# Rows of the quantised FFN's scales by way of DRAM, and another plan of rounds, in a two-layer decoder on one core

## The chip, the core and the metric

The kernel runs on one core of a Trainium2 chip. The metric is the time of one execution on the device in microseconds (us), from runs of the whole kernel. A core has five engines that work side by side, each through its own list of instructions in a fixed order: PE (matrix products), DVE (vector work), ACT (activation functions and copies), POOL (a slower vector engine) and SP (here: it issues DMAs). They wait for one another by semaphores. SBUF is the memory on the chip with 128 partitions, PSUM the one that PE writes to, DRAM the memory outside.

## What is computed

The reference is a decoder of two layers on x of 32 batches x 128 tokens x 256 features. Layer 0 is self-attention, cross-attention to a context and a mixture of experts with two of eight experts per token. Layer 1 is a gated linear recurrence with an MLP (stages d and m below), attention between x and the context in both directions (stage e) and a quantised feed-forward network with a depthwise convolution (stage f). Only stage f is touched:

```python
def act_quant(x):
    scale = 127.0 / jnp.clip(jnp.max(jnp.abs(x), axis=-1, keepdims=True), 1e-05)
    return jnp.clip(jnp.round(x * scale), -128, 127) / scale
def bit_linear(x, w):                  # weight_quant makes w ternary, times a mean
    return jnp.einsum('bsd,hd->bsh', act_quant(x), weight_quant(w))
h = bit_linear(_layernorm(x), w1)      # 256 -> 1024 features
h = depthwise_conv1d(h.transpose(0, 2, 1), conv_w, conv_b)   # 3 taps along the tokens
x = x + bit_linear(silu(h.transpose(0, 2, 1)), w2)           # 1024 -> 256
```

Each token has a scale of its own, once for the input (a factor to undo it, dq) and once for the hidden features (a factor to apply, s).

## The kernel before

Layer 0 goes first, in three stages, until about 1300 us. Then `layer1` works through 16 units of two batches (U = 2, T = 256 tokens). A unit is a list of small steps (`gather`, `d_stats`, ..., `f_out`), which `PLAN` gives round numbers by hand, 0 to 89. A new unit starts every `STEP` = 11 rounds, so that at any time up to nine units are at work in different steps. The loop at the end of `layer1` writes the program round by round, older units first; within what the data allow, the framework that builds the program then orders the instructions of DVE, ACT, POOL and SP, while matrix products keep the order of the program (`mm`, `turned`: lines 206 and 209). Each engine runs its list in order: a waiting instruction holds all behind it.

In stage f tokens lie along the free axis and features on the partitions, from `f_flip` on. A scale is computed with tokens on the partitions, 128 x 2 values (`scales`, lines 1007 to 1012). To multiply by it, the kernel needs the scales of all 256 tokens in a row, the same on every partition. `on_rows` does that on PE: for each of the two batches it multiplies the column, spread over 128 columns, with the identity matrix (tile rows_f), and ACT copies the result to SBUF (rows_f_sb, line 1021).

The steps of stage f, with the lines in the profile: `f_stats`, `f_norm` (1254 to 1259, ends with the first scale), `f_quant` (1265, 1267), `f_flip` (transposes, and the first row), then four pieces of two blocks of 128 features each: `f_h` (PE products with w1, then DVE line 1277: d_f = h_f times the row), `f_z` (ACT, 1282: the middle tap with the bias), `f_taps` (DVE, 1292: the left tap, for each block; ACT, 1296: the right tap's product e_f; POOL, 1298: its sum), `f_silu` (ACT, 1305), `f_top` (DVE, 1311 and 1316: the largest values over features within a partition, two pieces at once), `f_am` (PE transposes, DVE 1323, the second scale), `f_rows` (the second row), `f_round` (DVE, 1332: z_f times the row; 1333: rounding to zi_f) and `f_out` (PE, DVE 1346, then the store of the output on SP, 1349).

Other lines that the prediction names: the recurrence has its decay scan at 1117 and its state scan at 1123, between them POOL's product u_d (1091) and DVE's u_d (1122); then POOL's qn_d (1101), DVE's pre_d (1126), POOL's pre_d (1127), DVE's pre_d (1130) and yT (1132). Norms take a power on POOL (`rsqrt`, 956: rs_d, rs_m, rs_e, rs_f) with small DVE steps before (ve, ms: 954, 1054, 1055, 1144, 1145) and after (nb, 962). ACT applies them (xn 967, hn 974) and copies transposed tiles (hT, xT: 986). POOL adds x_m to x (1147). The softmax of stage e is nm_e (1212), exp (ACT, 1217), den_e (1223), at_e (1225), then lv_e (1238) and vv_e (1199). kv_e is loaded on SP (1176).

Of the kernel before, what the change touches and what calls it, by code (L numbers as in the profile page):

```python
# [10 lines left out]
F32 = mybir.dt.float32  # L11
# [3 lines left out]
ALU = mybir.AluOpType  # L15
AX = mybir.AxisListType

P = 128
S = 128
# [56 lines left out]
def decoder(ctx: ExitStack, tc: tile.TileContext, a: dict, out: bass.AP):  # L76
    nc = tc.nc
    V, A, PE, GP = nc.vector, nc.scalar, nc.tensor, nc.gpsimd
# [8 lines left out]
    dram = ctx.enter_context(tc.tile_pool(name="scratch", bufs=1, space=bass.MemoryType.DRAM))  # L87
    psp = ctx.enter_context(tc.tile_pool(name="ps", bufs=8, space=bass.MemoryType.PSUM))

    def bank(name, dt=F32):  # L90
        return psp.tile([P, 512 if dt == F32 else 1024], dt, tag="ps", name=name)
# [22 lines left out]
    def con(name):  # L114
        at, w = C_AT[name]
        return cst[:, at : at + w]

    ident, blk, pm = con("ident"), con("blk"), con("pm")
# [86 lines left out]
    def mm(out, lhsT, rhs, start, stop):  # L205
        tc.keep_in_program_order(PE.matmul(out, lhsT=lhsT, rhs=rhs, start=start, stop=stop))  # L206

    def turned(out, in_, by=None):
        tc.keep_in_program_order(PE.transpose(out, in_, ident if by is None else by))  # L209
# [12 lines left out]
    U = 2  # L222
    T = U * S
    NU = NB // U
    ckv = dram.tile([NU, P, 2, U * D], F32, name="ckv")
    rw = keepc.tile([P, 2, NB], F32, name="rw")
    slots = keepc.tile([P, 2, NB], I32, name="slots")
    wm = keepc.tile([P, 2], F32, name="wm")
# [645 lines left out]
    def ternary(wf, keep):  # L874
# [28 lines left out]
        (29, "m_out0"), (30, "m_out1 m_out2"), (31, "m_out3"), (32, "e_stats"), (33, "e_nb"),  # L903
        (34, "e_norm"), (36, "e_flip"), (39, "e_k e_v"), (45, "e_s"), (47, "e_exp"), (48, "e_soft"),
        (50, "e_at"), (53, "e_y"), (54, "f_stats"), (55, "f_norm"), (56, "f_quant"), (58, "f_flip"),
# [4 lines left out]
    )  # L910

    def layer1(wd):
# [4 lines left out]
        w1 = wq[:, 0, :].rearrange("p (c h) -> p c h", c=2)  # L917
# [3 lines left out]
        with tc.tile_pool(name="pl", bufs=1) as pool, tc.tile_pool(name="pl1", bufs=1) as keep:  # L921
# [10 lines left out]
            def sb(tag, name, bufs=1, dt=F32, shape=(2, T)):  # L932
                return pool.tile([P, *shape], dt, tag=tag, name=name, bufs=bufs)

            def flat(t):
                return t.rearrange("p a b -> p (a b)")

            def bank3(name, n=T):
                return bank(name)[:, : 2 * n].rearrange("p (a b) -> p a b", a=2)

            def sm(tag, name, w=U, bufs=3):
                return small.tile([P, w], F32, tag=f"l_{tag}", name=f"{tag}_{name}", bufs=bufs)
# [34 lines left out]
            def flipped(src, dst, n, dt=F32):  # L977

                pt = bank(f"pt_{n}", dt)[:, : 2 * T]
                for c in range(2):  # L980
                    for i in range(U):
                        turned(
                            pt[:, c * T + i * S : c * T + (i + 1) * S], src[:, i, c * P : (c + 1) * P],
                            ident if dt == F32 else ident_b,
                        )
                A.copy(flat(dst), pt)
                return dst

            def halves(w, m, xT, name):

                p = bank3(name)
                for e in range(2):
                    for c in range(2):
                        mm(p[:, e, :], w[:, c, (m + e) * P : (m + e + 1) * P], xT[:, c, :], c == 0, c == 1)
                return p
# [9 lines left out]
            def scales(am, k, name):  # L1005

                V.tensor_scalar(am, am, 1e-5, None, ALU.max)
                s = sm(f"qs{k}", name)
                V.reciprocal(s, am)
                V.tensor_scalar(s, s, 127.0, None, ALU.mult)  # L1010
                dq = sm(f"dq{k}", name)
                V.tensor_scalar(dq, am, 1.0 / 127.0, wm[:, k : k + 1], ALU.mult, ALU.mult)
                return s, dq

            def on_rows(v, k, name):

                p = bank(name)[:, :T]
                for i in range(U):
                    mm(p[:, i * S : (i + 1) * S], v[:, i : i + 1].to_broadcast([P, P]), ident, True, True)
                r = pool.tile([P, T], F32, tag=f"rows{k}", name=f"{name}_sb", bufs=2)  # L1020
                A.copy(r, p)
                return r[:, None, :].to_broadcast([P, 2, T])

            def unit(u):
                x = X[u * U // G][:, u * U % G : u * U % G + U, :]
                d_, m_, e_, f_ = f"d{u}", f"m{u}", f"e{u}", f"f{u}"
                o = {}
# [223 lines left out]
                def f_norm():  # L1251
                    o["xf"] = xn = sb("xf", f"xn_{f_}")
                    for i in range(U):
                        V.tensor_scalar(
                            xn[:, i, :], x[:, i, :], o["mv"][:, i, 0:1], o["rs"][:, i : i + 1],
                            ALU.subtract, ALU.mult,
                        )
                    am = sm("am", f_)
                    V.tensor_reduce(am, xn, AX.X, ALU.max, apply_absolute_value=True)
                    o["s1"], o["dq1"] = scales(am, 0, f_)  # L1260

                def f_quant():
                    xn = o["xf"]
                    for i in range(U):
                        V.tensor_scalar(xn[:, i, :], xn[:, i, :], o["s1"][:, i : i + 1], MAGIC, ALU.mult, ALU.add)
                    o["xi"] = sb("xi", f"xi_{f_}", 2, BF16)
                    V.tensor_scalar(flat(o["xi"]), flat(xn), MAGIC, 127.0, ALU.subtract, ALU.min)

                def f_flip():
                    o["hT"] = flipped(o["xi"], sb("xTf", f"xT_{f_}", 2, BF16), f_, BF16)  # L1270
                    o["rows1"] = on_rows(o["dq1"], 1, f"rows1_{f_}")

                def f_h(k):
                    if k == 0:
                        o["z"] = sb("z", f"z_{f_}", 3, shape=(NHC, T))
                    o["d", k] = sb("d", f"d_{f_}_{k}", 4)
                    V.tensor_tensor(o["d", k], halves(w1, 2 * k, o["hT"], f"h_{f_}_{k}"), o["rows1"], ALU.mult)  # L1277

                def f_z(k):
                    for j in range(2):  # L1280
# [37 lines left out]
                def f_am():  # L1318
                    pt = bank3(f"am_{f_}", S)
                    for i in range(U):  # L1320
                        turned(pt[:, i, :], o["top"][:, 0, i * S : (i + 1) * S])
                    am = sm("am2", f_)
                    V.tensor_reduce(am, pt, AX.X, ALU.max)
                    o["s2"], o["dq2"] = scales(am, 1, f_)

                def f_rows():
                    o["rows2"] = on_rows(o["s2"], 2, f"rows2_{f_}")
                    o["zi"] = sb("zi", f"zi_{f_}", 2, BF16, (NHC, T))

                def f_round(k):  # L1330
                    z = o["z"][:, 2 * k : 2 * k + 2, :]
                    V.tensor_tensor(z, z, o["rows2"], ALU.mult)
                    V.tensor_scalar(
                        flat(o["zi"][:, 2 * k : 2 * k + 2, :]), flat(z), MAGIC, MAGIC, ALU.add, ALU.subtract
                    )
# [16 lines left out]
                for k in range(4):  # L1352
                    for of in (gather, m_fc, m_out, f_h, f_z, f_taps, f_silu, f_top, f_round):
                        pieces[f"{of.__name__}{k}"] = partial(of, k)
                return pieces

            units = [unit(u) for u in range(NU)]
            pieces = {r: names.split() for r, names in PLAN}
            for t in range(STEP * (NU - 1) + PLAN[-1][0] + 1):
# [92 lines left out]
def program(arrays):  # L1452
    import concourse.bacc as bacc

    nc = bacc.Bacc("TRN2", target_bir_lowering=False, num_devices=1)
    args = {
        k: nc.dram_tensor(f"in_{k}", v.shape, mybir.dt.from_np(v.dtype), kind="ExternalInput").ap()
        for k, v in arrays.items()
    }
    out = nc.dram_tensor("out", arrays["x"].shape, F32, kind="ExternalOutput").ap()  # L1460
    with tile.TileContext(nc) as tc:
        decoder(tc, args, out)
    return nc
# [9 lines left out]
```

## Time and profile before

| | us |
|---|---|
| median of 3 runs (lowest to highest) | 2037.29 (2035.19 to 2041.46) |
| profiled execution, its own time | 2041.52 |
| its span, first to last instruction | 2039.4 |
| busy: PE, weight loads, DVE, ACT, POOL | 1807.9, 1477.4, 1166.9, 1080.8, 421.9 |
| layer 1, with its pipeline full: time between a unit and the next | 40.0 |
| row products on PE, all units (64 + 64 instructions of 328 and 286 ns) | 12.6 + 10.3 |
| row copies on ACT (32 of 371 ns) | 11.9 |

A profile is one execution. Durations of single instructions come from it, and sums of them are to be set against its span of 2039.4 us, which is 2.1 us less than that execution's time and 2.1 us above the median. Lines of the profile name the line of the program, the engine, the operation and the tiles (out<-in, without the numbers of buffers), then how many there are; a group adds its busy time, the mean duration in ns of one instruction, and the time that its engine idled just before with what ended it. A line of a wait view reads: waiting engine, tile and line <- what it waited for: us in total, how many times, the longest.

### The profile page before, as it was taken

To read this page: it belongs to the slowest core of one execution; us is meant where nothing else is said; L and a number is where in the kernel's file an instruction comes from. 1 tells how busy PE (TensorE), PEld (TensorE's weight loads), DVE (VectorE), ACT (ScalarE), POOL (GpSimd) and SP (SyncE) were. 2 spreads that over 40 slices of the span, in tenths; PEclk is the share of its full clock that TensorE was granted. 3 is DMA by queue.
4 is the path that set the end of the run, shared out by engine and by line. 5 is a ranking of instruction groups with operands and counts; after the bars stand their busy time and mean duration, and the time that the engine had idled before them with its cause. 6 is when DMAs were issued, how large, how long until landed. Compare 5 with 4: busy or idle time off the path is not lost.

```text
span 2039.4 us, 35437 instructions
## 1 busy us (share of the span) xinstructions
PE 1807.9 (89%) x13432; PEld 1477.4 (72%) x13432; DVE 1166.9 (57%) x3716; ACT 1080.8 (53%) x2584; POOL 421.9 (21%) x445
## 2 busy tenths in 40 slices
PE   6999999899986799999999995379989999999863
PEld 4777766676665478888888885268878887888752
DVE  6877667787777512101111111454677888888787
ACT  4454548888885422222222221235677777777662
POOL 4100000000000111111111102852333333333221
PEclk8999999998998899999999998689999999999976
DMA  4000010111002845555546553310000000000000
GB/s 155 3 2 3 8 38 22 33 33 52 16 19 75 325 174 180 202 192 187 211 173 210 183 189 120 87 49 11 11 11 27 16 17 21 27 16 21 27 11 21
DMA packets 51517, 162.13 MB, mean 79 GB/s; under 512 B 5392, under 2 KB 32144, under 8 KB 46224
## 3 DMA queue, kind: packets, MB, share of 16 engines
q1 hardware_dynamic: 44816, 141.99, 19.6%
q0 software_dynamic: 6528, 17.83, 3.1%
q8 instruction: 108, 1.77, 0.4%
q14 instruction: 65, 0.53, 0.1%
HBM read 132.80 MB, written 27.00 MB: 78 GB/s over the span
## 4 chain that ended last, share of the span: by engine, by line
PE 51%; DVE 26%; ACT 10%; POOL 6%; issue 4%; DMA 3%; SPq 0%; POOLq 0%; DVEq 0%; ACTq 0%
PE h L206 12%; PE y L206 12%; ACT sd_b L531 4%; PE od_a L206 3%; DVE top_f L1311 3%; DVE sd_b L518 2%; POOL z_f L1298 2%; PE st_a L206 2%; PE m_m L206 2%; PE et_b L209 2%; PE f_m L206 1%; DMA yr<-ys,slots 1%; DVE rd_a L497 1%; DVE nm L444 1%; PE q_a L206 1%
## 5 line engine op out<-in xcount | busy, mean ns | idle before, releaser
L820 ACT ACTIVATE hTs<-h,moe 128x256 f32<-128x256 f32 x288 | 136.3, 473 | 374.5 <-PE h L206 374.5
L206 PE MATMUL h<-xTs,moe 128*128 128x256 f32 x1152 | 254.7, 379 | 1.0 <-issue 1.0
L206 PE MATMUL y<-moe,hTs 128*128 128x256 f32 x1152 | 254.6, 379 | 0.0
L206 PEld LDWEIGHTS h<-xTs,moe 128*128 128x128 f32 x1152 | 218.7, 190 | 30.9 <-issue 1.2
L206 PEld LDWEIGHTS y<-moe,hTs 128*128 128x128 f32 x1152 | 216.2, 190 | 27.9
L531 ACT ACTIVATE sd_b<-sd_b,nan_b 128x128 f32<-128x128 f32 x512 | 173.8, 387 | 28.9 <-DVE nan_b L525 28.7
L795 POOL DMA_INDIRECT xr<-xs,who x72 | 68.3, 948 | 469.6 <-PE xs L209 426.8
L808 DVE COPY xTs<-xs 128x512 f32<-128x512 f32 x36 | 24.9, 690 | 236.1 <-PE xs L209 236.1
L832 DVE TENSOR_TENSOR yt<-y,moe 128x256 f32<-128x256 f32 x72 | 30.5, 424 | 215.7 <-PE y L206 215.7
L206 PE MATMUL m_m<-wd,sT_m 128*128 128x256 f32 x512 | 119.4, 381 | 0.0
L206 PE MATMUL f_m<-hT_m,wd 128*128 128x256 f32 x512 | 116.9, 383 | 0.0
L518 DVE CUSTOM_DVE_ANT_0 sd_b<-nd_b,s_b 128x128 f32<-128x128 f32 x512 | 113.0, 278 | 5.4 <-PE s_b L206 5.4
L1298 POOL TENSOR_TENSOR z_f<-z_f,e_f 128x508 f32<-128x508 f32 x64 | 70.7, 1104 | 197.3 <-ACT e_f L1296 110.1
L206 PEld LDWEIGHTS f_m<-hT_m,wd 128*128 128x128 f32 x512 | 96.4, 193 | 12.9 <-issue 0.5
L206 PEld LDWEIGHTS m_m<-wd,sT_m 128*128 128x128 f32 x512 | 95.8, 192 | 12.6 <-ACT sT_m L1158 0.2
L497 DVE RECIPROCAL rd_a<-od_a 128x256 f32<-128x256 f32 x32 | 56.0, 1751 | 63.2 <-PE od_a L206 63.2
L1282 ACT ACTIVATE z_f<-d_f,pv 128x256 f32<-128x256 f32 x128 | 70.3, 590 | 35.7 <-DVE d_f L1277 35.6
L544 POOL COPY dens_b<-den_b 128x256 f32<-128x256 f32 x32 | 12.8, 399 | 363.6 <-DVE den_b L542 202.3
L1292 DVE SCALAR_TENSOR_TENSOR z_f<-d_f,pv,z_f 128x254 f32<-128x254 f32 x128 | 64.1, 509 | 37.6 <-ACT z_f L1282 36.7
L474 ACT ACTIVATE et_a<-st_a 128x512 f32<-128x512 f32 x128 | 66.4, 614 | 27.6 <-PE st_a L206 27.6
L444 DVE TENSOR_REDUCE nm<-s_a 128x4 f32<-128x512 f32 x128 | 79.0, 680 | 2.6 <-PE s_a L206 2.6
L206 PE MATMUL s_b<-kEO_b,qT_b 32*128 32x256 f32 x512 | 53.3, 435 | 22.9 <-ACT kEO_b L313 17.0
(358 smaller groups left out, 4007.2 us busy)
## 6 DMA issues: line engine op xcount, KB each, us to landing
moe<-in_moe SPq DMA_DIRECT2D x36, 2180.0 KB, 8.6
ys<-yt SPq DMA_DIRECT2D x36, 256.0 KB, 2.3
ckv<-kv SPq DMA_DIRECT2D x8, 1024.0 KB, 5.2
kv_e<-ckv SPq DMA_DIRECT2D x16, 512.0 KB, 3.6
x<-in_x SPq DMA_DIRECT2D x8, 512.0 KB, 8.8
cT_b<-in_ctxT SPq DMA_DIRECT2D x8, 512.0 KB, 3.8
xs<-xn_c SPq DMA_DIRECT2D x8, 512.0 KB, 3.0
cT_k<-in_ctxT SPq DMA_DIRECT2D x8, 512.0 KB, 7.1
```

The lines of the kernel that those rows point to most:

```text
L206: tc.keep_in_program_order(PE.matmul(out, lhsT=lhsT, rhs=rhs, start=start, stop=stop))
L444: V.tensor_reduce(nms[i % 2][:, at : at + 2 * (P - HD)].rearrange("p (e x) -> p x e", e=2)[:, :2, :], sp[r], AX.X, ALU.max, negate=True,)
L474: A.activation(et[:, r].rearrange("p j q -> p (j q)"), st[r], AF.Exp)
L497: V.reciprocal(rd, od[:, 2 * S :])
L518: V.tensor_tensor_reduce(sd[:, r, j, :], nd[:, i, :], sp[r][:, j, :], SLOPES[head(r, j)], -3e38, ALU.add, ALU.max, mx[:, 4 * r + j : 4 * r ...
L531: A.activation(sd[:, r, j, :], sd[:, r, j, :], AF.Exp, bias=nan[:, 4 * r + j : 4 * r + j + 1], accum_out=den[:, h : h + 1] if r % 2 else None,
L795: GP.indirect_dma_start(out=xr[h], out_offset=None, in_=xs[:, :], in_offset=bass.IndirectOffsetOnAxis(ap=who[:, q : q + 1], axis=0),)
L820: A.activation(hT[:, hc, :], p[:, :TS], AF.Relu, bias=b1[:, hc : hc + 1])
L1282: A.activation(o["z"][:, hc, :], o["d", k][:, j, :], AF.Identity, scale=cw[:, hc, 1:2], bias=cb[:, hc : hc + 1],)
L1292: V.scalar_tensor_tensor(z[:, :, 1:], d[:, j, :].rearrange("p (b t) -> p b t", b=U)[:, :, : S - 1], cw[:, hc, 0:1], z[:, :, 1:], ALU.mult, ...
L1298: GP.tensor_tensor(z[:, :, : S - 1], z[:, :, : S - 1], e.rearrange("p h (b t) -> p (h b) t", b=U)[:, :, 1:], ALU.add,)
L1311: V.tensor_reduce(o["top"][:, k, :], o["z"][:, 4 * k : 4 * k + 4, :].rearrange("p h t -> p t h"), AX.X, ALU.max, apply_absolute_value=True,)
```

## The change

The rows of 14 of the 16 units go through a DRAM tensor `aside`; the two last units keep the products on PE. For a scale of 128 x 2 values, SP stores it (128 pieces of 8 bytes, one per partition) and, once that store has landed, loads the 1 KB back to all 128 partitions. In DRAM the two batches of a token lie side by side, so the row that is read alternates between them; `f_h` and `f_round` read it through a view with a stride of two words (`by_batch`). The transfers are issued in `f_norm` and `f_am`, where the scales are made, and no longer in `f_flip` and `f_rows`.

The plan of stage f is another for all units: from `f_norm` (55) to `f_h0` there are seven rounds instead of five, from `f_am` to `f_round0` six instead of four. The first and last rounds, `STEP` and the other stages are as they were. In the changed kernel the lines are moved down: 1117 is 1133, 1277 is 1296, 1292 is 1313, 1305 is 1326, 1311 is 1332, 1332 is 1356, 1333 is 1357, 1144 is 1160.

```diff
+    aside = dram.tile([NU, 2, S, U], F32, name="aside")
...
-        (60, "f_h0"), (62, "f_z0 f_h1"), (63, "f_z1 f_h2"), (64, "f_taps0 f_taps1 f_h3"),
-        (65, "f_silu0 f_silu1"), (66, "f_z2"), (67, "f_top0 f_z3"), (68, "f_taps2"), (70, "f_silu2"),
-        (71, "f_taps3"), (72, "f_silu3"), (73, "f_top1"), (75, "f_am"), (78, "f_rows"),
-        (79, "f_round0 f_round1 f_round2"), (81, "f_round3"), (89, "f_out"),
+        (62, "f_h0"), (63, "f_z0"), (64, "f_taps0 f_h1"), (65, "f_silu0"), (66, "f_z1"), (67, "f_h2"),
+        (68, "f_taps1 f_h3"), (70, "f_silu1 f_z2"), (71, "f_top0 f_z3"), (72, "f_taps3"),
+        (73, "f_taps2 f_silu3"), (74, "f_silu2 f_top1"), (78, "f_am"), (80, "f_rows"),
+        (84, "f_round0 f_round1"), (86, "f_round2 f_round3"), (89, "f_out"),
...
+            def by_dram(u):
+                return u < NU - 2
+
+            def on_rows(v, k, u):
+                r = pool.tile([P, T], F32, tag=f"rows{k}", name=f"rows{k}_f{u}", bufs=2)
+                if by_dram(u):
+                    nc.sync.dma_start(out=aside[u, k - 1], in_=v)
+                    nc.sync.dma_start(
+                        out=r, in_=aside[u, k - 1].rearrange("s i -> (s i)").partition_broadcast(P)
+                    )
+                    r = r.rearrange("p (s i) -> p i s", i=U)
+                else:
...
+                    r = r.rearrange("p (i s) -> p i s", i=U)
+                return r[:, None, :, :].to_broadcast([P, 2, U, S])
+
+            def by_batch(t):
+                return t.rearrange("p a (i s) -> p a i s", i=U)
...
+                    if by_dram(u):
+                        o["rows1"] = on_rows(o["dq1"], 1, u)
...
-                    V.tensor_tensor(o["d", k], halves(w1, 2 * k, o["hT"], f"h_{f_}_{k}"), o["rows1"], ALU.mult)
+                    V.tensor_tensor(
+                        by_batch(o["d", k]), by_batch(halves(w1, 2 * k, o["hT"], f"h_{f_}_{k}")), o["rows1"], ALU.mult
+                    )
...
+                    if by_dram(u):
+                        o["rows2"] = on_rows(o["s2"], 2, u)
...
-                    V.tensor_tensor(z, z, o["rows2"], ALU.mult)
+                    V.tensor_tensor(by_batch(z), by_batch(z), o["rows2"], ALU.mult)
```

More of the change, by code (lines that the diff above doesn't have):

```diff
@@ L1013, in scales @@
                 return s, dq
[L1015 to L1022, printed above, removed]
+            def by_dram(u):
[9 more added lines that the diff above has]
+                else:
+                    p = bank(f"rows{k}_p{u}")[:, :T]
+                    for i in range(U):
+                        mm(p[:, i * S : (i + 1) * S], v[:, i : i + 1].to_broadcast([P, P]), ident, True, True)
+                    A.copy(r, p)
+                    r = r.rearrange("p (i s) -> p i s", i=U)
+                return r[:, None, :, :].to_broadcast([P, 2, U, S])
+            def by_batch(t):
+                return t.rearrange("p a (i s) -> p a i s", i=U)
             def unit(u):
@@ L1270, in f_flip @@
                     o["hT"] = flipped(o["xi"], sb("xTf", f"xT_{f_}", 2, BF16), f_, BF16)
-                    o["rows1"] = on_rows(o["dq1"], 1, f"rows1_{f_}")
+                    if not by_dram(u):
+                        o["rows1"] = on_rows(o["dq1"], 1, u)
                 def f_h(k):
@@ L1324, in f_am @@
                     o["s2"], o["dq2"] = scales(am, 1, f_)
+                    if by_dram(u):
+                        o["rows2"] = on_rows(o["s2"], 2, u)
                 def f_rows():
-                    o["rows2"] = on_rows(o["s2"], 2, f"rows2_{f_}")
+                    if not by_dram(u):
+                        o["rows2"] = on_rows(o["s2"], 2, u)
                     o["zi"] = sb("zi", f"zi_{f_}", 2, BF16, (NHC, T))
```

## The prediction, made before the changed kernel ran

> **What bounds the kernel now.** I read the busy table by stage first, then the waits and the chain of one stretch, then single POOL and DVE instructions.
>
> The stages (columns: stretch, then busy us and number of instructions of PE, PEld, DVE, ACT, POOL; clock; DMA share; GB/s):
>
> ```profile
> 1559.00:1599.00 40.00, 38.05 (x208) 32.35 (x207) 33.60 (x87) 29.53 (x58) 15.19 (x13) 1.00 0.07 20
> 1599.00:1639.00 40.00, 38.14 (x207) 32.45 (x206) 33.61 (x88) 29.53 (x58) 15.19 (x13) 1.00 0.07 20
> ...
> 1877.00:1917.00 40.00, 33.64 (x191) 28.96 (x190) 33.72 (x83) 27.49 (x54) 12.33 (x10) 0.94 0.08 27
> ```
>
> Layer 1 repeats every 40 us once its pipeline is full (11 rounds, one unit). PE is busy 38.1 of 40, so it looks like the bound. The chain of waits between two such marks says otherwise:
>
> ```profile
> 1639.55 1.96 DVE top_f L1311
> ...
> 1642.66 0.46 ACT at_e L1217 x2
> 1643.12 0.48 ACT v_d L1089
> ...
> 1643.67 3.50 POOL u_d L1091
> ...
> 1654.44 0.60 ACT z_f L1282
> ...
> 1656.89 1.10 POOL z_f L1298
> ...
> 1658.01 0.63 ACT z_f L1305
> ```
>
> No PE line stands in it: DVE, ACT and POOL hand one another the conv and the recurrence, each in its fixed order. DVE's waits over six repeats (1599.52 to 1839.4):
>
> ```profile
> DVE z_f L1292 <- ACT z_f L1282: 16.5, 18, 1.6
> DVE pre_d L1130 <- POOL pre_d L1127: 8.3, 6, 1.4
> DVE u_d L1122 <- POOL u_d L1091: 4.6, 4, 1.2
> DVE top_f L1311 <- ACT z_f L1305: 2.8, 6, 0.5
> DVE xn_f L1254 <- POOL rs_f L956: 2.1, 6, 0.4
> ```
>
> Together 34.3, or 5.7 us per repeat. One more loss shows only in durations (groups of the same stretch):
>
> ```profile
> L1055 DVE TENSOR_TENSOR ms_d<-ms_d,mv_d 128x2 f32<-128x2 f32 x6 | 6.4, 1073 | 0.2
> L1316 DVE TENSOR_TENSOR top_f<-top_f 128x256 f32<-128x256 f32 x6 | 6.4, 1072 | 0.0
> L1145 DVE TENSOR_TENSOR ms_m<-ms_m,mv_m 128x2 f32<-128x2 f32 x6 | 1.0, 161 | 0.2
> L1091 POOL TENSOR_TENSOR u_d<-u_d,v_d 128x512 f32<-128x512 f32 x6 | 16.5, 2756 | 22.4 <-ACT v_d L1089 22.4
> ```
>
> Two instructions of two elements each take 161 and 1073 ns. The slow one meets POOL's z_f (L1298); u_d takes 1.28 us when it goes first and 3.49 us when L1332 and L1333 do. A blocked DVE costs 0.91 us (L1055), 0.65 (L1316, 418 ns elsewhere) and 0.35 (L1333: 4 x (505-418) ns), 1.9 us per repeat. So DVE's own work is 40.0-5.7-1.9 = 32.4 us.
>
> [...] The trace has no 8-byte store; its 256 KB stores land in 2.1 us. [...] No run here shows a stride of 2.
>
> **The change, part by part.**
>
> *Removed.* In 14 of 16 units two row products on PE (0.66 and 0.61 us in the timeline at 1640.96 and 1676.84) and two copies on ACT (L1021, 2 x 0.37 us). PE's load falls to 36.9 us per repeat. Neither is in the chain above, so by themselves they are worth 0 there. If PE sets the end, up to 1.3 us.
>
> *Added.* 56 DMAs on SP: per unit and scale a store of 128 pieces of 8 bytes and a load of 1 KB to 128 partitions, which waits on SP for the store. Behind it in SP's queue stand the output store and the next kv_e load; neither is urgent (kv_e is used 13 rounds of 3.6 us later). I price each between 2.1 us (out<-x) and 3.6 (kv_e), so the pair between 4.2 and 7.2. The first scale has some 30 us until d_f uses it. The second is tight: the changed kernel's DVE order has only d_f, top_f, a tap, u_d, the scan and at_e between its making and its first use, 7.4 us by the walk below, and the instruction after it waits 0.7 us or more longer for another thing. I take 0. From the slowest small load in the trace (sel, 2 KB, 8.1 us) plus 3.6, it would expose some 3.6 us per repeat: the upper end.
>
> *Strided operand.* L1277 and L1332 read every second word of the rows. [...] Upper end: the 1 KB stride of L1311 costs 1.95 us for 1024 elements, 1.9 ns each against 1.28 for L1259; half as much again on 8 x 0.68 us is 2.7 us per repeat. Neither has a lower end under 0: the count of elements is the same.
>
> *The plan*, the large item. I walked one repeat, from one decay scan (L1117, L1133 in the changed kernel) to the next, through the four engines in the built order, with the durations of the trace. DVE's work stays 32.4 us. Its waits become:
> - nb_d now follows ve_d with the POOL power (0.70 us) between: 0.9.
> - the first tap of piece 2 meets POOL's u_d (1.27 us), and u_d waits for that: 1.1.
> - den_e waits for the second exp: 0.6. pre_d waits for qn_d, itself held off POOL by the first round (0.68): 1.4. The next pre_d waits for POOL (1.27), which zi and a round hold off: 1.3.
> - top_f of the second half: POOL must add pieces 3 and 2 (2 x 1.09), and both stand against two L1332 and two L1333 (1.95 us), which exclude them. Whoever is first, top_f starts 1.95+2.2+0.65 (silu) after the tap, where DVE's own work there is 1.95+0.6 (lv_e): 2.3.
> - taps of piece 0 come straight after d_f of piece 0, with ACT's 0.6 between: 0.7. Before, yT covered it.
> - ms_m meets POOL's x add (1.27), which follows the piece 0 add (1.09): 1.1.
> - taps of piece 1 wait for ACT's z, which stands behind hn_m x2 and hT_d, and these behind rs_m, the x add and the piece 0 add on POOL: 1.6.
> - xn_f waits for rs_f, now behind the piece 1 add on POOL: 1.1. nb_e: 0.2.
>
> Sum 12.3, so a repeat takes 32.4+12.3 = 44.7 us against 40.0. If the exclusions cost nothing (less 0.7, 0.6, 0.6, 2.3 and, of ms_m, 0.6), 39.9. PE, at 36.9, then has 8 us of slack and hides behind DVE.
>
> Eight repeats are full (scans at 1555.2 to 1875.7): 8 x 4.7 = +37.6. The filling (1440 to 1555) has PE busy 37.7 of 40 us at first, then partly the new waits: +2 (-3 to +6). In the draining (1877 to 2039) DVE idles 34 us, in which the new waits partly vanish, but the last unit's conv is interleaved later: +5 (-5 to +15). The two last units keep PE rows: 0.
>
> Span 2039.4+37.6+2+5 = 2084.0, plus 2.1 around it (2041.52 against 2039.4) = 2086.1. The profiled execution is 4.2 above the median 2037.29, so 2082 in terms of the median.
>
> **Rivals.**
> - *Slower by the walk*: 2082, own range 2058 to 2105. For: the built order and the 161 against 1073 ns. Against: small shifts decide who goes first.
> - *Faster, PE as the bound*: PE at 38.1 of 40 us is what holds the others, and DVE's waits move with it. The repeat falls to 36.9 plus PE's idle 1.85 = 38.7. 8 x -1.3, and -4 in the PE-bound filling: 2023. It decides if DVE's waits and blocked time in the new order stay under 40.0-32.4 = 7.6 us. Against: no PE line in the chain.
> - *Next to nothing*: the exclusions fall kindly, the repeat stays near 40, the ends add some 7: 2044.
> - *The store is late*: the small pieces expose 3.6 us per repeat on top of the walk: 2110 to 2130. For: no such store in the trace. [...]
>
> **How the numbers follow.** Chances: walk 0.72, next to nothing 0.10, faster 0.11, late store 0.07. A measurement of this kernel tells some 0.3% (6 us) from no change, so 2031 to 2043 is the same. The nothing case splits in halves between same and slower: faster 0.11, same 0.05, slower 0.84. Leaving out the faster and same cases and the top of the late store gives 2044 to 2108.
>
> **What would show it.** In the changed profile: full repeats of 44 to 45 us instead of 40; PE busy share down and no PE line in the chain; DVE waits for ACT's z before L1313 and for L1326 before L1332 grown to 2 us and more; ms_m (L1160) at 1 us instead of 0.15; POOL's z_f adds above 1.09 us. It is wrong if repeats are under 40 with PE lines in the chain, or if the first rounds (L1356) wait for a DMA, or if L1296 and L1356 take clearly over 0.68 us.

## The result, and the profile after

The changed kernel takes 2085.91 us (median of 4 runs, 2084.07 to 2087.09), beside 2039.38 for the kernel before (2035.19 to 2042.67): a ratio of 1.0229, with a 95% interval of 1.0213 to 1.0244. It is slower, by 46.5 us. The forecast was 2082.

I read the new profile in the order of the prediction. First the stages: two full repeats, then two pairs of repeats (columns as before: stretch, busy us and instructions of PE, PEld, DVE, ACT, POOL; clock; DMA share; GB/s).

```profile
1603.54:1647.81 44.27, 39.71 (x200) 33.85 (x199) 35.25 (x89) 28.97 (x56) 14.99 (x13) 0.92 0.10 24
...
1736.52:1825.25 88.73, 79.43 (x398) 67.68 (x397) 70.60 (x175) 57.93 (x111) 30.14 (x26) 0.92 0.14 25
```

A repeat takes 44.3 us where it took 40.0, though PE has 8 products fewer in it (198.4 matrix products per repeat over five repeats, 206.4 before). Two numbers stand out. DVE is busy 35.3 us per repeat; its own work was put at 32.4. And PE's clock reads 0.92 in a stretch where it read 1.00 before.

DVE's waits over five repeats (1603.54 to 1825.25):

```profile
DVE z_f L1313 <- ACT z_f L1303: 11.4, 10, 1.6
DVE top_f L1332 <- ACT z_f L1326: 10.4, 5, 2.1
DVE pre_d L1142 <- POOL qn_d L1117: 5.8, 5, 1.2
DVE xn_f L1270 <- POOL rs_f L957: 5.6, 5, 1.1
DVE nb_d L963 <- POOL rs_d L957: 4.4, 5, 0.9
DVE den_e L1239 <- ACT at_e L1233: 4.0, 5, 0.8
DVE x L1370 <- PE o_f L206: 1.0, 5, 0.2
```

No line here waits for a DMA (waits under 0.1 us are not listed). The lost time that shows only in durations (groups of the same five repeats):

```profile
L1319 POOL TENSOR_TENSOR z_f<-z_f,e_f 128x508 f32<-128x508 f32 x20 | 31.5, 1582 | 68.3 <-ACT e_f L1317 37.5 <-DVE ve_f L955 21.7 <-DVE z_f L1313 9.1
L1313 DVE SCALAR_TENSOR_TENSOR z_f<-d_f,pv,z_f 128x254 f32<-128x254 f32 x40 | 23.2, 599 | 11.4 <-ACT z_f L1303 11.4
L1356 DVE TENSOR_TENSOR z_f<-z_f,rows_f 128x512 f32<-128x512 f32 x20 | 18.7, 952 | 0.2
L1160 DVE TENSOR_TENSOR ms_m<-mv_m 128x2 f32<-128x2 f32 x5 | 5.2, 1044 | 0.2
```

Blocked time has moved: ms_m, two elements, now takes 1.04 us (0.15 before), the taps L1313 take 599 ns a piece (480), the rounds L1356 952 (680). That is 0.89 + 8 x 0.12 + 4 x 0.27 = 2.9 us per repeat, about what DVE's 35.3 has above the 32.4 (which also holds the short gaps between instructions, so that the two are not quite the same thing).

Last the chain of waits, one repeat of it (start us, us, what):

```profile
1605.15 1.76 PE o_f L206 x16
...
1606.94 0.88 DVE x L1370 x2
...
1608.77 0.60 ACT z_f L1303
...
1616.95 1.37 POOL qn_d L1117
...
1623.81 2.74 issue
1626.55 1.09 POOL z_f L1319
...
1628.33 1.94 DVE top_f L1332
...
1635.20 1.05 DVE ms_m L1160
...
1636.79 0.72 POOL rs_m L957
1637.53 0.91 ACT hn_m L975 x2
1638.43 0.48 ACT hT_d L987
...
1638.96 3.78 PE q_d L206 x8
1642.74 2.78 PE a_d L206 x8
```

The 2.74 us of "issue" lie within POOL's first add (L1319, piece 3): it begins at 1623.51 and lasts 3.08 us, where an add alone takes 1.09, while DVE runs two rounds with their roundings (1623.69 to 1625.63); the second follows at 1626.55. Then the chain runs as the prediction walked it: top_f, ms_m, rs_m, hn_m, hT_d. What the prediction did not have is the end: from hT_d the chain goes through PE (q_d, a_d, k_d, g_d, o_f) and back to DVE's x.

Where the 45.0 us between the two spans arose, by the decay scans (L1117, L1133): up to unit 7's scan +4.3 (1559.43 against 1555.16), the eight full repeats +34.7 (355.3 against 320.6, that is 44.41 against 40.07 each), after unit 15's scan +6.0 (169.7 against 163.7).

### The profile page after: what moved, and what is told of

Same layout as the page of the kernel before. It is cut to its first block, busy times and chain, and to the rows that moved or that the text cites. A ratio compares the mean times of both kernels' runs of the same rounds, so it can differ in the third digit from the quotient of the medians.

```text
span 2084.4 us, 35276 instructions
## 1 busy us (share of the span) xinstructions
PE 1817.4 (87%) x13320; PEld 1483.7 (71%) x13320; DVE 1187.7 (57%) x3716; ACT 1071.6 (51%) x2556; POOL 428.4 (21%) x445
## 4 chain that ended last, share of the span: by engine, by line
PE 55%; DVE 21%; ACT 10%; issue 5%; DMA 4%; POOL 4%; SPq 0%; POOLq 0%; DVEq 0%; ACTq 0%
PE h L206 12%; PE y L206 12%; ACT sd_b L532 4%; PE od_a L206 3%; DVE sd_b L519 2%; PE q_d L206 2%; PE st_a L206 2%; PE m_m L206 2%; DVE top_f L1332 2%; PE et_b L209 1%; DMA yr<-ys,slots 1%; DVE z_f L1313 1%; DVE z_f L1356 1%; PE a_d L206 1%; DVE rd_a L498 1%
## 5 line engine op out<-in xcount | busy, mean ns | idle before, releaser
L1319 POOL TENSOR_TENSOR z_f<-z_f,e_f 128x508 f32<-128x508 f32 x64 | 90.7, 1424 | 237.9 <-DVE z_f L1313 90.0
L1326 ACT ACTIVATE z_f<-z_f 128x512 f32<-128x512 f32 x64 | 40.3, 629 | 107.0 <-POOL z_f L1319 106.9
L206 PE MATMUL q_d<-hT_d,wd 128*128 128x256 f32 x128 | 51.2, 569 | 50.4 <-ACT hT_d L987 50.4
L1313 DVE SCALAR_TENSOR_TENSOR z_f<-d_f,pv,z_f 128x254 f32<-128x254 f32 x128 | 69.7, 562 | 28.4 <-ACT z_f L1303 28.3
```

The source lines that it names most:

```text
L1313: V.scalar_tensor_tensor(z[:, :, 1:], d[:, j, :].rearrange("p (b t) -> p b t", b=U)[:, :, : S - 1], cw[:, hc, 0:1], z[:, :, 1:], ALU.mult, ...
L1319: GP.tensor_tensor(z[:, :, : S - 1], z[:, :, : S - 1], e.rearrange("p h (b t) -> p (h b) t", b=U)[:, :, 1:], ALU.add,)
L1326: A.activation(z, z, AF.Silu)
```

## The experiments

The table has all twelve runs and the two kernels. "Repeat" is an eighth of the time from unit 7's scan to unit 15's in the profiled execution, "drain" the time from there to the end of its span. The ratios are to runs of the kernel before that were taken alongside, with medians from 2038.7 to 2041.5.

| kernel | median us | ratio to before (95%) | repeat | unit 7's scan at | drain |
|---|---|---|---|---|---|
| before | 2039.4 | | 40.07 | 1555.2 | 163.7 |
| changed | 2085.9 | 1.0229 (1.0213 to 1.0244) | 44.41 | 1559.4 | 169.7 |
| e1 plan only | 2078.7 | 1.0183 (1.0166 to 1.0200) | 43.68 | 1561.4 | 167.0 |
| e2 rows only | 2059.9 | 1.0094 (1.0075 to 1.0113) | 41.42 | 1561.5 | 166.1 |
| e3 late rounds | 2073.7 | 1.0163 (1.0145 to 1.0180) | 42.95 | 1560.2 | 168.4 |
| e4 late taps | 2055.3 | 1.0073 (1.0056 to 1.0090) | 40.89 | 1554.7 | 171.1 |
| e5 PE kept busy | 2103.4 | 1.0312 (1.0298 to 1.0326) | 44.19 | 1574.3 | 174.3 |
| e6 no add 1 | 2082.9 | 1.0208 (1.0192 to 1.0223) | 44.33 | 1558.6 | 169.3 |
| e7 both | 2089.6 | 1.0242 (1.0228 to 1.0256) | 43.50 | 1571.4 | 171.1 |
| e8 no adds 2, 3 | 2058.0 | 1.0093 (1.0079 to 1.0107) | 42.00 | 1556.9 | 163.1 |
| e9 first scale only | 2037.2 | 0.9987 (0.9979 to 0.9995) | 39.47 | 1557.6 | 163.3 |
| e10 eight rounds | 2044.0 | 1.0021 (1.0013 to 1.0028) | 40.75 | 1558.5 | 158.5 |
| e11 add on DVE | 2082.2 | 1.0209 (1.0196 to 1.0222) | 43.92 | 1559.6 | 170.1 |
| e12 nine rounds | 2041.5 | 1.0013 (1.0005 to 1.0021) | 40.73 | 1558.8 | 158.0 |

In e10 and e12 seven of the eight repeats last 40.3 to 40.6 us and the eighth 42.8 and 42.6; what it adds is more than made up in the drain.

My theory: the new order on DVE, ACT and POOL costs the time, and the way by DRAM is free. The rival: the way by DRAM costs it (late small pieces, strided rows). A second rival came from the profile after: PE's fallen clock is the loss.

**e1: the plan alone.**

```diff
-                return u < NU - 2
+                return False
```

> The changed kernel's plan, but all 16 units take their rows from PE, as before the change; nothing goes by way of DRAM, and the row tiles are contiguous. The pipeline's order on POOL stays as in the changed kernel; on DVE one of four rounds moves up by some ten instructions. Theory (the plan's order on DVE, ACT and POOL costs the time): 2070 to 2090, a full repeat of 43 to 45 us. Rival (the way by DRAM costs it: late small pieces, strided rows): 2035 to 2050, a repeat near 40.

It took 2078.7 us with repeats of 43.7: the plan without any DRAM makes 37 of the 46.5 us. In its five repeats top_f (L1332) waits 5.2 us for ACT where the changed kernel waits 10.4; otherwise the same waits stand there with nearly the same sizes. That fits its one moved round, and its 1.0 us per repeat is enough for the 0.7 between the two. The rival is out as the main cause.

**e2: the rows alone**, with the plan of the kernel before in the changed kernel.

> The plan of the kernel before, with the rows of 14 units by DRAM. The built order moves a little with it (some rounds go ahead of the scan). Theory (the way by DRAM is free where nothing waits for it): 2025 to 2048, a repeat of 38.7 to 40.5. Rival (the way by DRAM costs it): 2065 to 2090, with the first round L1356 or the first d_f L1296 waiting for a DMA by 2 us and more per repeat.

It took 2059.9, between the two expectations: here I was wrong. The way by DRAM is not free under the old plan: the repeat grows by 1.3 us. DVE's waits over five repeats have two new lines at the top:

```profile
DVE z_f L1356 <- DMA rows_f<-aside: 10.3, 5, 2.4
DVE nb_d L963 <- POOL rs_d L957: 9.3, 5, 1.9
```

and the chain names what is late:

```profile
1633.94 2.98 DMA aside<-qs_f
1636.94 3.90 DMA rows_f<-aside
1640.86 0.69 DVE z_f L1356
```

Store and load of the second scale take 6.9 us together here (up to 7.6 in the five repeats), and four rounds cover only 4.8 of them. The order also moved: the first rounds went ahead of the scan, and ve_d to just ahead of nb_d, which brings the wait there. Other waits shrank, so the repeat does not grow by the sum of the two. The strided rows cost nothing: where DVE is not blocked, L1356 takes 684 ns here (median), 682 in e1 with rows that lie together.

**e3 and e4: half of the plan each**, rows by DRAM.

```diff
 # e3: f_h to f_top as before, then
-        (75, "f_am"), (78, "f_rows"), (79, "f_round0 f_round1 f_round2"), (81, "f_round3"),
+        (78, "f_am"), (80, "f_rows"), (84, "f_round0 f_round1"), (86, "f_round2 f_round3"),
 # e4: f_h to f_top as changed, then
-        (78, "f_am"), (80, "f_rows"), (84, "f_round0 f_round1"), (86, "f_round2 f_round3"),
+        (75, "f_am"), (78, "f_rows"), (79, "f_round0 f_round1 f_round2"), (81, "f_round3"),
```

> Half of the plan: f_h, f_z, f_taps, f_silu and f_top in the rounds of the kernel before, f_am to f_round in the later rounds of the changed one; rows by DRAM. Theory: of the new waits those at nb_d (0.9), pre_d (1.4 and up to 1.3) stay, those at top_f (2.3), at the taps of piece 0 (0.7) and at POOL's u_d (1.1) go: a repeat of 39.5 to 42.5, 2033 to 2060. Rival (the way by DRAM, or the late rounds as such, cost it): 2070 and more.

> The other half: f_h to f_top in the rounds of the changed kernel, f_am to f_round in those of the kernel before; rows by DRAM. Theory: POOL's adds of pieces 3 and 2 no longer meet the rounds, so the wait of top_f falls from 2.1 to under 1, those at ms_m (0.9), the taps of piece 1 (1.6) and xn_f (1.1) stay: a repeat of 39.5 to 42.5, 2033 to 2060. Rival (the way by DRAM costs it): 2070 and more.

e3 took 2073.7, outside what the theory gave this half and within the rival's 2070 and more: here too the way by DRAM is not free. It has f_am at 78, as the changed kernel, and its first round waits for the DMA all the same (five repeats):

```profile
DVE z_f L1356 <- DMA rows_f<-aside: 10.7, 5, 2.6
```

With the old taps there is less DVE work between the scale and the first round: 5.2 us, where the changed kernel has 7.1 to 7.2. So the six rounds of the changed plan cover the pair only together with its later taps. The taps, too, wait longer for ACT than the theory had it, 4.4 us per repeat against 2.3 in the changed kernel. e4 took 2055.3, as expected in time and not in its reason: top_f does not wait less, but more (12.7 us in five repeats, against 10.4), though no round stands near POOL's two adds there. In its chain, ACT's queue (e_f, xn_d, then L1326) leads up to it. So with the last taps just ahead of it, top_f is late even without rounds beside the adds. In the changed kernel the rounds do lengthen POOL's add (3.08 us), and in e1, where one of them has moved up, the wait is half; but taking them all away brings ACT's queue in their place.

**e5, e6, e7: PE's clock and the second path.** The changed kernel's PE idles ahead of q_d, and runs q_d and a_d slowly (five repeats):

```profile
L206 PE MATMUL q_d<-hT_d,wd 128*128 128x256 f32 x40 | 18.9, 655 | 23.2 <-ACT hT_d L987 23.2
L206 PE MATMUL a_d<-hT_d,wd 128*128 128x256 f32 x40 | 15.0, 545 | 0.0
```

In the kernel before (also five repeats) PE idles 0.4 us there:

```profile
L206 PE MATMUL q_d<-hT_d,wd 128*128 128x256 f32 x40 | 10.0, 392 | 1.8 <-ACT hT_d L986 1.8
L206 PE MATMUL a_d<-hT_d,wd 128*128 128x256 f32 x40 | 9.4, 379 | 0.0
```

By their busy time, 33.9 us against 19.4 in five repeats, that is 2.9 us per repeat, in the chain itself. e5 puts products ahead of m_out2 to keep PE busy; e6 leaves out one POOL add on DVE's own path; e7 does both.

```diff
 # e5, e7: in m_out
+                    if k == 2:
+                        for _ in range(8):
+                            mm(o["m"][:, 1, :], ident, win[:, 0, :D], True, True)
 # e6, e7: in f_taps
+                    if k != 1:
                         GP.tensor_tensor(
...
```

> The changed kernel with eight extra fp32 products of 128x256 on PE ahead of m_out2, whose result the real product overwrites; they fill most of PE's idle 4.6 us ahead of q_d. The order on DVE, ACT and POOL is that of the changed kernel. Theory (the waits of DVE, ACT and POOL set the repeat; x waits for PE's o_f by only 0.2 us): 0 to -0.3 us per repeat, 2082 to 2087. Rival (the new idle time lets PE's clock fall, and the q_d and a_d that then take 0.65 and 0.55 us a product in place of 0.39 and 0.38 are the loss, 2.9 us per repeat): 8 x -2.9 = -23, some 2063.

> The changed kernel without POOL's add of the third tap in piece 1 (L1319 for k = 1 is left out; the conv of that piece lacks one tap). Orders are else unchanged. The wait of xn_f for rs_f (1.1 us per repeat) goes. Theory with DVE alone as the path: 8 x -1.1 = -9, 2077. Theory with two paths of nearly one length from hT_d to x (DVE's own, and PE's q_d, a_d, k_d, g_d, o_f at the lower clock): x then waits for o_f by 1.1 to 1.3 us instead, and the time stays at 2084 to 2087.

> The two edits before together: no add of the third tap in piece 1 (left out of the conv), and eight extra products on PE ahead of m_out2. Theory with two paths: PE's part is 2.9 us shorter, so that taking 1.1 us off DVE's part now counts: 8 x -1.1 = -9 and up to 0.3 per repeat more, 2074 to 2078. Rival (PE's clock has no part in it): the same as without the products.

e5 took 2103.4, outside both. The stretch that the expectation spoke of did as the theory said: repeats of 44.19 us, 0.2 less. PE idles 2.7 us there on average. In three of the eight repeats q_d takes 392 ns, in five 597 to 654, and these repeats last 44.05 and 44.28 us on average: PE's speed alone makes little difference. The time is lost elsewhere: eight products are 3.0 us per unit, and while the pipeline fills, PE is the bound (busy 39.8 of the 40 us from 1440 us on): unit 7's scan comes 14.9 us later and the drain is 4.6 us longer. I had not counted that.

e6 took 2082.9, just under the 2084 to 2087 of two paths, with repeats of 44.33: taking 1.1 us of DVE's waits away gained 0.1. The wait of xn_f is gone, and another of the same size has come, for a product of PE by way of ACT (five repeats):

```profile
DVE al_d L1095 <- ACT al_d L1093: 5.6, 5, 1.2
```

So there are two paths of one length from hT_d to the end of the repeat, DVE's and PE's. (I had named x as the place; it is al_d, made from a_d.) e7 took 2089.6, not the expected 2074 to 2078, since it pays for the extra products in filling and draining as e5 does; but it is 13.8 us faster than e5. With PE's part shorter, the same edit counts: repeats of 43.50 against 44.19 in e5, 0.7 us less, of 1.1 expected. The first six of its full repeats are 0.9 shorter than e5's, the last two as long. What e5 gives back of PE's speed is thus worth 0.2 us per repeat by itself; without it, nearly all that an edit on DVE's path brings stays hidden. One rival is untested: in the changed kernel PE's granted clock falls every 44.37 us, which is 13 of the 3.41 us pieces that the clock record is made of, and e6, with a mean clock of 0.92 as well, has repeats of 44.33. Whether that spacing holds the repeat at its length, more than two paths that happen to be equal, no run tells.

**e8: no adds in pieces 2 and 3.**

```diff
+                    if k < 2:
                         GP.tensor_tensor(
...
```

> The changed kernel without POOL's adds of the third tap in pieces 2 and 3 (left out of the conv). Orders are else unchanged. The wait of the second top_f (L1332) for ACT's silu goes. Theory: -2.1 us per repeat, 8 x -2.1 = -17, some 2069; x goes on waiting for o_f by about 0.2, since the gain lies ahead of hT_d and so shortens both paths. Rival (another wait takes its place, such as d_f_0 or the taps of piece 0, or the time is the DMA's): less than half of it, 2078 and more.

It took 2058.0, 28 us less. The wait of top_f is gone from the list, and the repeat is 2.4 us shorter, of 2.1 expected. The drain shrinks by 6.6 us, to 163.1, about what the kernel before has. So the two adds and the wait that they bring, ahead of hT_d and so on both paths, are over half of the loss in this order. With them gone the rounds wait a little for the DMA, 1.2 us in five repeats.

**e11: x + x_m on DVE.**

```diff
-                    GP.tensor_tensor(x, x, o["x1"], ALU.add)
+                    V.tensor_tensor(x, x, o["x1"], ALU.add)
```

> The changed kernel with x + x_m (L1163) on DVE in place of POOL, at the same place in the order; it computes the same. Theory: ms_m (1.04 us) falls to 0.15, rs_m and with it hn_m and hT_d come 0.9 us earlier, and the added 0.68 us of DVE lie where DVE waited 1.6 us for ACT: -0.9 us per repeat, some 2077 to 2079. Rival (DVE is simply the fullest engine of the chain, so that its work counts): +0.68 us per repeat, 2091.

It took 2082.2, less gain than the theory had, and no loss as the rival had. ms_m falls to 161 ns as expected. The repeat falls by 0.5, of 0.9 expected, to 43.9. The add stands ahead of ms_m in the order that was built, so its 0.66 us delay rs_m, and the taps of piece 1 go on waiting 1.6 us. POOL's block is worth what it measures only if nothing takes its place.

**e9, e10, e12: the way by DRAM with the old taps.** e9 sends only the first scale by DRAM. e10 and e12 send both, leave f_am at 75 and move only the rounds.

```diff
 # e10
-        (79, "f_round0 f_round1 f_round2"), (81, "f_round3"), (89, "f_out"),
+        (83, "f_round0 f_round1 f_round2"), (84, "f_round3"), (89, "f_out"),
 # e12
-        (79, "f_round0 f_round1 f_round2"), (81, "f_round3"), (89, "f_out"),
+        (84, "f_round0 f_round1"), (86, "f_round2 f_round3"), (89, "f_out"),
```

> The plan of the kernel before; only the first scale's rows (14 units) go by DRAM, the second's come from PE as before. The built order is that of the kernel before but for two neighbours that change places. Theory (the way by DRAM is free where it has 30 us of cover, and PE's 0.65 and ACT's 0.37 us saved are not in the chain): 2030 to 2042, a repeat of 39.3 to 40.2. Rival (the way by DRAM costs it): 2050 and more.

> Both scales' rows by DRAM, the plan of the kernel before with f_round0 to 2 at round 83 and f_round3 at 84 in place of 79 and 81, so that the second scale has eight rounds; f_h to f_am as before. Of the new waits of the changed kernel none is left by the built order. Theory: no wait of L1356 for a DMA in full repeats, a repeat of 39.3 to 40.5, 2030 to 2048. Rival (late rounds or the way by DRAM cost it): 2065 and more.

> Both scales' rows by DRAM, the plan of the kernel before with the rounds of the changed kernel for f_round (84 and 86), f_am at 75: nine rounds for the second scale. Against the run with f_am at 78 this moves the store 3 rounds up and leaves the rest. Theory: the DMA wait of that run (2.1 us per repeat) goes and the taps wait no longer behind it: a repeat of 39.5 to 41.5, 2033 to 2055. Rival (the late rounds cost it): 2065 and more.

All three times came out as the theory said. e10's repeat of 40.75 lies just above its range: den_e now waits 2.2 us per repeat for ACT, so the built order did not leave out every new wait. e12 differs from e3 only in f_am, three rounds earlier: the wait for the DMA is gone from its full repeats, the repeat falls from 42.95 to 40.73, the time from 2073.7 to 2041.5. e9 has repeats of 39.47, 0.6 under the kernel before, and is the only version below it: 0.9987 (0.9979 to 0.9995), a gain of some 2.6 us that is smaller than the 0.3% which I took as the limit. Whether the 0.6 come from PE's and ACT's saved row or from neighbours in DVE's order that changed places, no run tells apart.

## Why the prediction was right, and where it was not

*The size of the plan's part* came out of the walk nearly item by item. Per repeat, predicted and measured in the profile after:

| item | predicted | measured |
|---|---|---|
| nb_d for rs_d | 0.9 | 0.9 |
| first tap of piece 2 behind POOL's u_d | 1.1 | 1.0 (blocked taps) |
| den_e | 0.6 | 0.8 |
| pre_d for qn_d | 1.4 | 1.2 |
| next pre_d for POOL | 1.3 | 1.1 (as a blocked L1356) |
| top_f, second half | 2.3 | 2.1 |
| taps of piece 0 | 0.7 | 0.7 |
| ms_m behind POOL's x add | 1.1 | 0.9 |
| taps of piece 1 | 1.6 | 1.6 |
| xn_f for rs_f | 1.1 | 1.1 |
| nb_e; x and al_d | 0.2; 0 | 0; 0.3 |
| sum | 12.3 | 11.7 |

The measured items are waits of the list over five repeats, divided by 5 (the 11.4 of L1313 split by its two sizes, 0.67 and 1.61 in the timeline), and blocked time from durations. 32.4 + 11.7 = 44.1 against 44.4 found. The eight repeats were put at +37.6 and measured +34.7.

*Filling and draining*: +2 and +5 predicted, +4.3 and +6.0 measured. The drain is right in part by luck: e1, without DRAM, has only +3.3; the other 2.7 come with the way by DRAM, where three rounds of the drain wait 4.6 us for the DMA, which the prediction put at 0. In the filling, unit 5's scan is 6.4 us earlier than before and unit 7's 4.3 later, so that the small net is two larger effects. The total of +45.0, against 44.6 predicted, owes part of its precision to errors of opposite sign (-2.9, +2.3, +1.0).

*What was removed*, taken as worth 0: e9 leaves room for up to 0.6 us per repeat for the first scale. Small, and hidden in the changed kernel.

*The 56 DMAs*, taken as 0: right in the full repeats of the changed kernel, with nothing to spare. In its five repeats the pair takes 6.8 to 7.2 us from the scale on, at the upper end of the estimate of 4.2 to 7.2, and the cover is 7.1 to 7.2, not 7.4: the first round starts 0.02 to 0.27 us after the load has landed. In the drain the rounds do wait for it. And it was right only with the changed plan: in e2 and e3 the first round waits 2.1 us per repeat. The late-store rival was closer than 0.07 says.

*The strided operand*, taken as 0 on an estimate of mine that no run had shown: right, 684 ns (e2) against 682 (e1). By the letter, L1356 at a mean of 952 ns was one of the prediction's signs of being wrong; but its median in the changed kernel is 682, and the mean comes from single rounds that POOL blocks (1.76 us beside pre_d), not from the stride.

*"No PE line in the chain"* was wrong, as was PE's "8 us of slack". The step that failed took PE's load as a sum at full clock. In the changed order q_d waits 4.6 us for hT_d, and after that idle time PE runs slowly: its granted clock reads 0.50 for 6.83 us of each repeat, and q_d takes 655 ns a product against 392 in the kernel before, where PE waits 0.4 us there. In e4, with waits of at most 2.0 us, it takes 544. PE's q_d to o_f then ends only 0.2 us after DVE would need it. For this forecast it cost 0.2 us; for judging what a single wait is worth it decides (e6).

*The reason for top_f's 2.3 us* was half right. Size and place are (2.1; e8), but the prediction counted it among what the exclusions cost (DVE and POOL instructions lengthen where they meet, as POOL's add of 1.09 us becomes 3.08), and in e4 the wait is there without rounds beside the adds, by way of ACT's queue. The figure of 39.9 for a repeat without exclusions was too kind for that reason.

*The blocked instructions* moved where the walk put them: 2.9 us per repeat, 1.9 before. The walk took for granted that other pairs of DVE and POOL instructions behave as those seen in the profile before (161 against 1073 ns); that was an estimate, and ms_m beside POOL's x add bears it out (1044 ns; 161 in e11, where that add is on DVE). The 1.9 leaves out at_e, at 443 ns a piece before and 283 after, so that the 32.4 of DVE's own work is some 0.3 too high.

## What to carry to other kernels

Where no engine is full, a new order could be priced here by walking one repeat through all queues with measured durations: one engine's own work and its waits add up to the length of the repeat. But this sum is not a list of gains, since a second path may lie 0.2 us below (e6: 1.1 us taken away, 0.1 gained). A transfer that replaces a cheap computation has to be given its cover where the order is least sensitive: moving only the consumer (e12) cost 0.13%, moving everything between cost 2.3%. Work that fills an engine's idle time in one stage is paid in another where that engine is the bound (e5).

## What the runs showed of the hardware that I had not expected

PE's granted clock fell beside short gaps. From 1440 us to the drain the clock record of the two kernels has only 1.00 and 0.50, in pieces that are multiples of 3.41 us. In the changed kernel it reads 0.50 for 6.83 us of each full repeat, with gaps of 4.6 to 4.9 us ahead of q_d: in the repeat of the chain above the gap ends at 1638.96 us, the clock has read 0.50 since 1637.92, and q_d takes 655 ns a product. In the kernel before, gaps of 0.3 to 0.4 us leave it at 1.00 (392 ns), and so do e2's five gaps of 8.2 us in all, the longest 1.9 (392 ns). In e4 five gaps of 10.0 us in all, the longest 2.0, go with a mean clock of 0.96 over five repeats, and q_d takes 544 ns. The length of the gap alone does not decide: e5's five gaps are longer, 13.5 us in all, and its q_d takes 537 ns, a mean that mixes both speeds. By what rule the clock falls no run tells.

A store of 128 pieces of 8 bytes lands after 2.7 to 3.3 us (medians of the two scales in the changed kernel), where the output's 256 KB take 2.4; the load of the same 1 KB to 128 partitions takes 3.9 (median).
